# Smaller booked times for VectorE in a kernel whose instruction order is made by a planner

## The chip, the cores and the metric

The kernel runs on one core of one Trainium2 chip. The time is device microseconds of one execution; the median of several executions is given, and one further execution was taken by the hardware profiler. A core has the engines TensorE (PE in the profile; its weight loads are PEld), VectorE (DVE), ScalarE (ACT), GpSimd (POOL) and SyncE (SP, which here only issues DMAs). Each engine works off its own queue in order and waits on semaphores where it needs another engine's result. So the order in which a program writes its instructions into the queues is part of its speed.

## The reference

A block of a Flamingo model: gated cross-attention of `x` (4 x 256 x 512) to a context (4 x 1601 x 512), with 32 query heads in 8 groups of 4, head size 128, and then a gated feed-forward layer with eight low-rank experts of which two are used. All in float32.

```python
def xattn(query, kv, Wq, bq, Wkv, bkv, Wo, bo):      # 32 heads, 8 kv heads, HDIM = 128
    q = (query @ Wq + bq).reshape(B, L, NKV, G, HDIM)
    k_, v_ = jnp.split(kv @ Wkv + bkv, 2, axis=-1)
...
    scores = jnp.einsum('blkgd,bmkd->bkglm', q, k) * scale
    attn = jax.nn.softmax(scores, axis=-1)
    o = jnp.einsum('bkglm,bmkd->blkgd', attn, v).reshape(B, L, NHEAD * HDIM)
    return o @ Wo + bo

def ffn(x, base_W, router_W, lora_A, lora_B):        # E = 8, R = 16, TOP_K = 2
    base = jnp.einsum('bsd,od->bso', x, base_W)
    probs = jax.nn.softmax(jnp.einsum('bsd,ed->bse', x, router_W), axis=-1)
    top_vals, top_idx = jax.lax.top_k(probs, TOP_K)
...
    mid = jnp.einsum('bsd,edr->bser', x, lora_A) * w_dense[..., None]
    return base + jnp.einsum('bser,erd->bsd', mid, lora_B) * SCALING

x = x + jnp.tanh(g_xattn[0]) * xattn(layernorm(x), ctx_4096, ...)
x = x + jnp.tanh(g_ffn[0]) * ffn(layernorm(x), ...)
```

## The kernel before

**Tiles.** The work runs over 4 batches, 8 head groups of each, and 2 blocks of 128 queries of each group: 64 tiles. A tile (`key` = batch, head group, query block) has 4 heads x 128 queries = 512 columns. Its 1601 keys come as 13 row tiles: the remainder of 65 rows first, then six pairs of 128 rows, so 7 pieces `j` in all.

**One tile.** For each piece `score_unit` (L1109 on) writes the score product `sc` (L1138), ScalarE's copy of it from its bank into `p` (L1147), and VectorE's running maximum, by `fold`: the first pair of pieces by L1067, the short piece by L1070, the others by L1073. Then `softmax` (L1160 on) writes the spread of the maximum over the partitions (`spread`, L1078 on: L1102, L1103, L1085, L1086, L1087, L1093, L1096) and puts into queues, for each piece, the subtraction of the maximum (VectorE, L1177), the exponential (ScalarE, L1180) and the running sum (VectorE, again `fold`). `av_unit` writes the product `av` with the values (L1229); `normalize` (L1288) multiplies by the reciprocal of the sum; the output product `po` (L1306), or its seven-product form `pox`, `poy`, `poz` (L484, with VectorE's additions into `xa`, L490), follows.

`run_group(cur, prev)` alternates the score pieces of one tile with the `av` pieces of the tile before it. Between two such groups `window` fills in other work: the projections of queries, keys and values of later head groups (`pair_steps`, seven products in place of eight, names `pxq`, `pxk`, `pxv` and so on, with ScalarE's copies L941 and L944 and VectorE's additions in `add_to`, L951), the sums of weights which these products need (`weight_sums`, L351: S1, then S2 from S1, then S4 from S2, and S3 from none of them), the output products, the transposition of the next batch's context (`ctx_steps`, with VectorE's L723), and near the end the feed-forward layer.

**The planner.** The program that writes the queues keeps a clock for each engine: `clock["now"]` for TensorE, `clock["v"]` for VectorE, `clock["a"]` for ScalarE, in nanoseconds of its own reckoning. Each VectorE instruction is booked with a figure. Where it is written at once, `vec(ns)` adds the figure to `clock["v"]`; where it goes to a queue, `later(queue, "v", ns, ready, fn, key)` stores it, and `take` adds it when the piece is written. Behind a booked end `SEM` = 200 ns are added before another engine is reckoned to see the result (`done[key]`), and a PSUM bank is given back (`give`) at such a time.

Decisions made from these clocks:

- `spend` moves TensorE's clock and calls `pump`, which writes all queued pieces whose booked start lies before it; `fit` writes queued pieces that would be over by a given time, with 300 ns of tolerance (`FIT`); `force` writes what is needed for a key, with pieces in front of it that fit (1200 ns for subtractions).
- `window` picks among the tasks by when their inputs and a bank are booked to be ready. After `softmax` a time `clock["hold"]`, which is 1500 ns behind the booked end of the spread less three score products, sets up to when ready tasks are taken as filler.
- `score_unit` takes one of nine `p` buffers, whose former content must have been summed (`force(("sum", ...))`).

No figure is seen by the chip: each instruction is the same whatever is booked for it, and the semaphores guard each dependence. SP's queue is written in the same pass: `keep` stores summed weights (behind VectorE's sums), `load_pair` and `load_wo` load the next ones, booked at 6000 ns.

## Time and profile before

| what | value |
|---|---|
| median of 3 runs | 2561.35 us (2560.31 to 2561.53) |
| the profiled execution's own time | 2559.67 us |
| its span, first to last instruction | 2557.9 us |
| granted TensorE clock | 1.000 |
| VectorE busy, 1800 to 2400 us | 530.63 of 600 us |
| ScalarE busy, 1800 to 2400 us | 286.77 of 600 us |
| TensorE busy, 1200 to 1800 us | 600.00 of 600 us |

Mean durations of the VectorE groups whose booked figures change, as the groups by line and shape give them:

| line, operation | count | mean ns of one |
|---|---|---|
| L1073, maximum of a pair, 128x1024 | 252 | 1224 |
| L1073, sum of a pair, 128x1024 | 252 | 1221 |
| L1067, first maximum, 128x1024 | 63 | 1221 |
| L1070, short piece, 65x512 | 64 | 689 |
| L1177, subtraction, 65x512 | 64 | 672 |
| L1288, normalising, 128x512 | 64 | 684 |
| L351, weight sum of `wq`, 128x256 | 64 | 419 |
| L490, addition of `pox` to `xa`, 128x256 | 80 | 481 |
| L951, addition to `v`, 128x384 | 30 | 553 |

A mean duration is from an instruction's start to its end. The distance from one start to the next start can be shorter or longer than that, and is read from a timeline. A timeline's row gives the start in us, the length in us, the engine, the line, the operation, out<-in, the shapes and how many instructions were merged into the row; in brackets stands the engine's idle time before it and what ended it.

### The profile page before, as it was taken

To read this page: it belongs to the slowest core of one execution; us is meant where nothing else is said; L and a number is where in the kernel's file an instruction comes from. 1 tells how busy PE (TensorE), PEld (TensorE's weight loads), DVE (VectorE), ACT (ScalarE), POOL (GpSimd) and SP (SyncE) were. 2 spreads that over 40 slices of the span, in tenths; PEclk is the share of its full clock that TensorE was granted. 3 is DMA by queue.
4 is the path that set the end of the run, shared out by engine and by line. 5 is a ranking of instruction groups with operands and counts; after the bars stand their busy time and mean duration, and the time that the engine had idled before them with its cause. 6 is when DMAs were issued, how large, how long until landed. Compare 5 with 4: busy or idle time off the path is not lost.

```text
span 2557.9 us, 25738 instructions
## 1 busy us (share of the span) xinstructions
PE 2547.1 (100%) x9235; PEld 1486.4 (58%) x9235; DVE 2178.9 (85%) x3180; ACT 1188.1 (46%) x1899; POOL 74.4 (3%) x153
## 2 busy tenths in 40 slices
PE   9999999999999999999999999999999999999999
PEld 7557566565555656455565665756656455555544
DVE  4888898898889988999787787878788898888887
ACT  2544354445445554455444444444454445444451
POOL 0000000000000000000000000000000000000000
PEclk9999999999999999999999999999999999999999
DMA  4313222324110111012121111212221011110100
GB/s 158 122 64 108 87 102 78 113 85 149 48 56 23 44 52 56 25 39 83 50 80 37 62 52 62 81 48 81 86 83 56 26 51 52 52 50 30 49 1 33
DMA packets 75496, 167.13 MB, mean 65 GB/s; under 512 B 5372, under 2 KB 32028, under 8 KB 72808
## 3 DMA queue, kind: packets, MB, share of 16 engines
q1 hardware_dynamic: 74424, 164.41, 19.2%
q8 instruction: 73, 1.20, 0.2%
q0 software_dynamic: 416, 0.81, 0.1%
q14 instruction: 55, 0.45, 0.1%
q10 hardware_dynamic: 528, 0.26, 0.0%
HBM read 119.06 MB, written 46.40 MB: 65 GB/s over the span
## 4 chain that ended last, share of the span: by engine, by line
PE 98%; DVE 1%; DMA 0%; ACT 0%; issue 0%; SPq 0%; DVEq 0%
PE av L1229 28%; PE sc L1138 28%; PE pxk L896 6%; PE pxv L907 6%; PE pxq L896 4%; PE po L1306 3%; PE pyk L896 3%; PE pyv L907 3%; PE pox L484 3%; PE pyq L896 2%; PE pzk L896 2%; PE pzv L907 2%; PE poy L484 1%; PE pzq L896 1%; PE ptv L1020 1%; PE pv L847 1%
## 5 line engine op out<-in xcount | busy, mean ns | idle before, releaser
L1147 ACT COPY p<-sc 65x512 f32<-65x512 f32 x820 | 474.5, 586 | 658.9 <-PE sc L1138 592.1
L1138 PE MATMUL sc<-qT,kT 128*128 128x512 f32 (+1 forms) x1664 | 775.7, 592 | 0.0
L1229 PE MATMUL av<-p,v 65*128 65x512 f32 x1640 | 766.4, 592 | 2.4 <-ACT p L1180 2.4
L1229 PEld LDWEIGHTS av<-p,v 65*128 65x128 f32 x1640 | 309.2, 190 | 375.9 <-issue 367.7
L1138 PEld LDWEIGHTS sc<-qT,kT 128*128 128x128 f32 (+1 forms) x1664 | 307.0, 186 | 375.1 <-issue 342.2
L1177 DVE TENSOR_TENSOR p<-p,mb 65x512 f32<-65x512 f32 x442 | 484.4, 1137 | 0.2
L1073 DVE TENSOR_TENSOR mx<-mx,p 128x1024 f32<-128x1024 f32 x252 | 308.4, 1224 | 167.8 <-ACT p L1147 164.5
L1180 ACT ACTIVATE p<-p 65x512 f32<-65x512 f32 x442 | 421.1, 990 | 34.8 <-DVE p L1177 32.7
L1073 DVE TENSOR_TENSOR sm<-sm,p 128x1024 f32<-128x1024 f32 x252 | 307.6, 1221 | 8.6 <-DVE sm L1073 0.5
L1093 POOL COPY quadm_sm<-quadm_sm 32x16 f32<-32x16 f32 x124 | 66.0, 532 | 2302.6 <-DVE quadm_sm L1205 2298.8
L896 PE MATMUL pxq<-xq,wq 128*128 128x256 f32 x512 | 131.2, 379 | 0.0
L941 ACT ACTIVATE kT<-pxk,biasT 128x384 f32<-128x384 f32 (+1 forms) x120 | 58.0, 509 | 148.8 <-PE pxk L896 148.4
L896 PEld LDWEIGHTS pxq<-xq,wq 128*128 128x128 f32 x512 | 92.1, 189 | 30.3 <-issue 14.0
L941 ACT ACTIVATE qT<-pxq,biasT 128x256 f32<-128x256 f32 x64 | 30.3, 473 | 140.2 <-PE pxq L896 140.2
L896 PE MATMUL pxk<-T,wk 128*128 128x417 f32 (+1 forms) x240 | 90.4, 499 | 0.0
L907 PE MATMUL pxv<-wv,T 128*128 128x128 f32 x720 | 90.2, 275 | 0.0
L907 PE MATMUL pxv<-wv,ctxT 128*128 128x128 f32 x720 | 90.2, 275 | 0.0
L896 PE MATMUL pxk<-ctxT,wk 128*128 128x417 f32 (+1 forms) x240 | 90.0, 499 | 0.0
L907 PEld LDWEIGHTS pxv<-wv,ctxT 128*128 128x128 f32 x720 | 86.4, 192 | 4.2 <-issue 3.8
L907 PEld LDWEIGHTS pxv<-wv,T 128*128 128x128 f32 x720 | 86.3, 192 | 3.7 <-issue 3.3
L1067 DVE TENSOR_TENSOR mx<-p,p 128x1024 f32<-128x1024 f32 x63 | 76.9, 1221 | 12.7 <-ACT p L1147 12.1
L1306 PE MATMUL po<-wo,oT 128*128 128x512 f32 x176 | 78.5, 592 | 0.0
(264 smaller groups left out, 2674.2 us busy)
## 6 DMA issues: line engine op xcount, KB each, us to landing
wo<-in_L_xattn_Wo_dram SPq DMA_DIRECT2D x18, 1024.0 KB, 5.6
kept_q<-wq SPq DMA_DIRECT2D x16, 896.0 KB, 4.8
wq<-kept_q SPq DMA_DIRECT2D x16, 896.0 KB, 5.1
wo<-kept_wo SPq DMA_DIRECT2D x13, 1024.0 KB, 6.0
wk<-kept_k SPq DMA_DIRECT2D x11, 896.0 KB, 4.5
wv<-kept_v SPq DMA_DIRECT2D x11, 896.0 KB, 4.5
ctx<-in_ctx_dram SPq DMA_DIRECT2D x36, 256.0 KB, 2.7
wq<-in_L_xattn_Wq_dram SPq DMA_DIRECT2D x32, 256.0 KB, 3.1
```

Of the source, the lines that this page charges most:

```text
L484: nc.tensor.matmul(bk[:, :HD], left[i]()[:, c, :], blk[:, c, :], start=first and c == 0, stop=c == 1, skip_group_check=True,)
L896: nc.tensor.matmul(bk[:, :n], a(SLOT[i], c), operand(i, c, s, n), start=first and c == 0, stop=c == 1, skip_group_check=True,)
L907: nc.tensor.matmul(bk[:, t * HDIM : (t + 1) * HDIM], operand(i, c, s + t * P, P), a(SLOT[i], c), start=first and t == 0 and c == 0, stop=c ...
L941: nc.scalar.activation(dst, src, AF.Identity, bias=bias_of(kind, h0 + f))
L1067: nc.vector.tensor_tensor(acc, p[first], p[first + 1], op)
L1073: nc.vector.tensor_tensor(acc, acc, p[j], op)
L1138: nc.tensor.matmul(sc[:r, :], kT_t[b, h][:, key_col(i) : key_col(i) + r], qT_t[b, h][:, :, l * P : (l + 1) * P], start=True, stop=True,)
L1147: nc.scalar.copy(p[:r, k, :], sc[:r, :])
L1177: nc.vector.tensor_tensor(p, p, m, ALU.subtract)
L1180: nc.scalar.activation(p, p, AF.Exp, scale=scale)
L1229: nc.tensor.matmul(av, v_t[b, h][:r, i, :], p_t[key][j][:r, k, :], start=(j == 0 and k == 0), stop=(j == NPAIR - 1 and k == len(pairs[j]) ...
L1306: nc.tensor.matmul(po, oT_t[key][:, g, :], w_t["o", b, h][:, g, :], start=(g == 0), stop=(g == G - 1),)
```

## The change

Eight lines of booked figures become smaller. Nothing else in the program is touched.

```diff
@@ weight_sums
-                "T", "v", 420, clock["now"] + LAG_PAIR,
+                "T", "v", 345, clock["now"] + LAG_PAIR,
@@ block_out_steps
-                t = done[key] = vec(420)
+                t = done[key] = vec(405)
@@ add_to
-                t = vec(140 + 1.04 * src.free_size(), ready)
+                t = vec(75 + 1.04 * src.free_size(), ready)
@@ fold
-                return 1930
+                return 1870
...
-        return 1220
+        return 1150
@@ softmax
-            later("sub", "v", 1140 if n > 1 else 690, clock["v"], sub, ("sub", key, j))
+            later("sub", "v", 1140 if n > 1 else 600, clock["v"], sub, ("sub", key, j))
...
-            ns = 0 if j <= first else 1230 if j > first + 1 else 1970 if first else 1230
+            ns = 0 if j <= first else 1190 if j > first + 1 else 1870 if first else 1190
@@ sum_spread
-        later("norm", "v", 690, ("av", key), lambda: normalize(key), ("norm", key))
+        later("norm", "v", 610, ("av", key), lambda: normalize(key), ("norm", key))
```

The figures that `fold` returns are used for the maximum alone; for the sum the figures of `softmax` are booked. The figures of the spread, of the subtraction of a full pair (1140), of the sums over the context and of the block sums (L462) stay.

## The prediction

> **What bounds the kernel now.** I read the page's chain of waits first, then TensorE's waits alone, then the timelines of TensorE and VectorE. The chain ended last on TensorE for 98% of its length:

> ```profile
> PE 2547.1 (100%) x9235; PEld 1486.4 (58%) x9235; DVE 2178.9 (85%) x3180; ACT 1188.1 (46%) x1899; POOL 74.4 (3%) x153
> PE 98%; DVE 1%; DMA 0%; ACT 0%; issue 0%; SPq 0%; DVEq 0%
> ```

> Busy time alone could hide short stalls, since a matmul's recorded end overlaps the next. So I took TensorE's start-to-start distances: a 512-column matmul follows another after a median 429 ns (3,611 of them), 256 columns 216 ns (1,560), 417 columns 349 ns (444), 384 columns 322 ns (452), 128 columns 112 ns (3,074), 136 columns 115 ns (64). Counts times these medians, with the few smaller forms, are about 2541 us. TensorE ran from 1.05 to 2553.97, so 2553 us: some 12 us are not work, and 6 of them lie in the first 100 us. The listed waits agree:

> ```profile
> PE av L1229 <- ACT p L1180: 2.4, 2, 1.2
> PE pt_ctx L258 <- DMA ctx<-in_ctx_dram: 1.6, 2, 1.2
> PE warm L1791 <- DVE ones L1788: 1.1, 1, 1.1
> PE pk L803 <- ACT ctxT L260: 0.8, 1, 0.8
> PE pk L803 <- DVE ctxT L264: 0.6, 1, 0.6
> PE su L1253 <- DVE sm L1073: 0.3, 1, 0.3
> PE pmt L1540 <- DVE tail_w L1529: 0.2, 1, 0.2
> ```

> The columns are the total, the count and the longest, in us. 7.0 us in all. The reader is to see how little any new order can win: only the first two rows (without 0.4 us at 6.06) and the last two lie after the start-up, 4.1 us together. By start-to-start distances they are 4.9, and 5.1 with 0.2 in front of a block product at 2047.

> How far VectorE's work lies ahead of TensorE is the second thing. An `av` product needs the exponentials of its tile, made by VectorE's subtraction (L1177) and ScalarE's exponential (L1180). A tile in the middle of the run:

> ```profile
> 1637.68 1.23 DVE L1073 TENSOR_TENSOR mx<-mx,p 128x1024 f32<-128x1024 f32 x1 [2.21 <-ACT p L1147]
> 1638.94 0.69 DVE L1102 TENSOR_TENSOR mx<-mx 128x512 f32<-128x512 f32 x1
> ...
> 1645.21 0.68 DVE L1288 TENSOR_TENSOR oT<-av,rb 128x512 f32<-128x512 f32 x1
> 1645.80 0.41 DVE L951 TENSOR_TENSOR qT<-pyq,qT 128x256 f32<-128x256 f32 x1
> ...
> 1649.95 3.49 DVE L1177 TENSOR_TENSOR p<-p,mb 128x1024 f32<-128x1024 f32 x3
> ...
> 1654.27 0.42 DVE L462 TENSOR_TENSOR xa<-xa,oT 128x256 f32<-128x256 f32 x1
> 1654.61 0.55 DVE L951 TENSOR_TENSOR v<-pyv,v 128x384 f32<-128x384 f32 x1
> ...
> 1660.99 3.88 DVE L1073 TENSOR_TENSOR sm<-sm,p 128x1024 f32<-128x1024 f32 x3
> ```

> and ScalarE and TensorE beside it:

> ```profile
> 1644.32 1.56 ACT L1180 ACTIVATE p<-p 65x512 f32<-65x512 f32 x2
> 1662.63 1.02 PE L1229 MATMUL av<-p,v 65*128 65x512 f32 x2
> ```

> The tile's exponentials begin at 1644.3, the product that reads the first starts at 1662.6. Pairing the n-th exponential with the n-th `av` over all 64 tiles, the first product's margin has a median of 12.8 us; only two tiles have none (0.05 us), the last tile has 1.35, one has 3.7, and the rest 6.5 or more. The two bare ones are here, with what stands before them:

> ```profile
> 1190.10 3.60 PE L1306 MATMUL po<-wo,oT 128*128 128x512 f32 x8
> 1193.78 2.74 PE L1138 MATMUL sc<-qT,kT 128*65 128x512 f32 x6
> 1197.72 1.12 PE L1229 MATMUL av<-p,v 65*128 65x512 f32 x2 [1.20 <-ACT p L1180]
> ```

> ```profile
> 2434.82 1.12 PE L1229 MATMUL av<-p,v 65*128 65x512 f32 x2 [1.20 <-ACT p L1180]
> ```

> **The change, part by part.** No instruction is added or removed; eight lines of figures by which the program's writer books VectorE's time become smaller. What the chip does changes only through the order in which instructions were written into the three queues. Engine work therefore changes by 0.

> How much is booked less, for one 128-row query tile of one head group: maximum, first pair 1930 to 1870 (60), four further pairs by 70 (280); short subtraction 690 to 600 (90); sums, first 1970 to 1870 (100), four more by 40 (160); normalising 690 to 610 (80). Together 770 ns; for 63 tiles 48.5 us, or 2% of VectorE's 2178.9 us. Beside this, 75 ns on each of 96 weight sums (7.2 us), 15 on each of 140 block additions (2.1 us), 65 on each of some 300 pair additions (20 us).

> Are the new figures near the distances? Independent neighbours: subtractions in the row of three stand (3.49 - 1.22) / 2 = 1.135 us apart with 1.22 each (booked 1140, unchanged); 1645.21 to 1645.80 is 0.59 (booked 610); 1654.27 to 1654.61 is 0.34 (booked 345). Dependent ones are longer: the three sums stand (3.88 - 1.22) / 2 = 1.33 us apart, booked 1190; 1637.68 to 1638.94 is 1.26, booked 1150, for the last maximum before its spread. A tile is thus under-booked by 4 x 0.14 + 0.11 = 0.67 us at the upper end; at the lower, with 1.26 for each sum, by 0.39. In the old booking the same sums gave 4 x 0.10 + 0.04 = 0.44 and 0.16.

> [...]

> Under-booking costs time only where TensorE arrives before the result. For the tiles' exponentials the margin hides it: 0.67 us against 3.7 or more for 61 of 64 tiles. With the cover gone it costs at most 0.67 us at each of three tiles, 2.0 us. I take 0.3, as the order at those places must also turn out worse for it to count. The weight sums are chains of three and one free operation: 0.45 us chained (1653.82 to 1654.27 in the same timeline, a pair of the same size) against 345, so two of them make the last one 0.21 late, and its own 0.42 of length is 0.07 over the figure; the writer adds 200 ns behind every VectorE result, which leaves 0.08. Were 0.21 bare in all 24 groups it would be 5.0 us; I take 0.1, since the row nearest to it, TensorE's waits, shows none today on a weight sum.

> Banks are given back earlier in the booking, so a matmul that reuses one can wait. A 384-column addition is booked at 474 + 200, and its row lasts 0.55: it still ends 0.12 before the booked time. Bounds: 0 to 0.1 us for each dependent step that loses its slack; I take 0.

> SP's queue is in order and stores the summed weights behind VectorE's last sum, with loads behind them. The stored and loaded weights take 4.5 to 6.0 us to land by the page's DMA rows, booked 6.0. A sum that is put later makes the loads late by as much, a microsecond at most (one 1.22 us operation in front); I take 0, as TensorE waits for no weight load today; bounds 0 to 1.2 for one place.

> The existing waits: bounds -4.1 (the two `av` waits and the context tile of 591.13, 1.37, 1.37 and 1.38 by start-to-start distances) to 0. What ends them is the real chain from the last maximum to the exponential, and a DMA, which no booked figure shortens; I take 0. At the end of the run, where one 0.75 us addition in front of the last routing chain moves the end: -0.2 to +0.7, taken 0.1.

> Sum: 0 + 0.3 + 0.1 + 0 + 0 + 0 + 0.1 = +0.5 us. The profiled execution took 2559.67 us (span 2557.9, 1.8 around it), so 2560.2; the median of the runs shown, 2561.35, is 1.7 above that execution, so 2561.9 is the forecast against the median.

> **The rivals.** First, slower: **the cover of the short windows is moved away.** The windows between tiles close when VectorE is booked to be done; booked earlier, they take less filler, and the order of the filler changes. At 1197.72 the wait is 1.37 us although eight `po` matmuls (3.43 us) stand before it; put elsewhere, the wait becomes 4.8. The other bare tile and the one with 3.7 us of margin (its `av` at 1089.64) are the further places. Two losses of 3.43 make +6.9, so 2568.2; three 2571.6. It decides from 5.1 us of lost cover. For it: filler is scarce exactly there. Against: filler that is not taken early remains for later windows, the total is the same, and 61 tiles have 3.7 us or more in hand.

> Second, faster: **the waits after the start-up close**, because saved filler reaches the bare tiles and the context load gets more lead. All of them are -5.1, so 2556.2; two of the three long ones are -2.7, 2558.6, which is still no difference. For it: each is a mere 1.4 us. Against: it needs every one of them and no new one.

> Third, the change does not do what it says: shifts of 15 to 90 ns are smaller than the tolerances of 300 and 1200 ns with which the writer fits pieces in, so TensorE's order is hardly touched: 2561.4.

> **How the numbers follow.** A measurement of this kernel tells about 0.2%, 5.1 us, from no change. No difference, my forecast and the third rival together: 0.75. Slower, by the first rival: 0.17. Faster, by the second: 0.08. The likeliest case's own range is 2556.2 to 2566.5. For 8 in 10 I cut its lower end to 2557.5, as two of three waits would have to close for less, and reach into the first rival to 2568.5, its price for two places.

> **What would show it.** VectorE's busy time stays at 2179 us within 3, with another order. TensorE's total listed wait stays between 4 and 11 us, and its start-to-start sum at 2541. The medians of the `av` margins shift by under 3 us. I am wrong if TensorE shows new waits of over 5 us in total on an exponential, a weight sum or a context tile, or if a tile with 6.5 us of margin today is bare; the first rival is shown by a shorter run of filler in front of a bare tile.

## The result, and the profile after

Over 21 runs each, the changed kernel takes 2565.2 us (2563.58 to 2566.35) and the kernel before 2559.99 us (2559.16 to 2562.89). The ratio is 1.0019, with a 95% interval of 1.0012 to 1.0025: slower by 5.2 us, clear of zero and about as large as the 0.2% that the prediction called no difference. The profiled execution of the changed kernel took 2565.99 us, its span is 2564.2, 6.3 more than before. One execution of the run `undo_w` below, the profiled one, was slow (2667.27 us at a granted clock of 0.948); the other ten of that run have a median of 2563.4 us.

The page's first and fourth part, of the kernel after:

```profile
PE 2552.2 (100%) x9235; PEld 1487.6 (58%) x9235; DVE 2179.4 (85%) x3180; ACT 1188.1 (46%) x1897; POOL 69.1 (3%) x153
PE 96%; DVE 2%; DMA 1%; ACT 0%; issue 0%; SPq 0%; DVEq 0%; ACTq 0%
```

The same instructions, the same VectorE time (2179.4 against 2178.9), and TensorE is still the chain. TensorE's waits, total, count and longest in us:

```profile
PE av L1229 <- ACT p L1180: 2.2, 2, 1.8
PE warm L1791 <- DVE ones L1788: 1.1, 1, 1.1
PE pt_ctx L258 <- DMA ctx<-in_ctx_dram: 0.9, 1, 0.9
PE pk L803 <- ACT ctxT L260: 0.8, 1, 0.8
PE pv L847 <- DMA wv_first<-in_L_xattn_Wkv_dram: 0.8, 1, 0.8
PE pk L803 <- DVE ctxT L264: 0.5, 1, 0.5
PE pyk L896 <- ACT kT L941: 0.5, 1, 0.5
PE av L1229 <- ACT p_last L1180: 0.4, 1, 0.4
PE pmt L1540 <- DVE tail_w L1529: 0.2, 1, 0.2
```

They sum to 7.4 us, 0.4 more than before. So this view does not show where 6.3 us went. Two things escape it: a wait that begins while the last matmul's recorded end still runs, and a matmul that is simply slower. Distances from one matmul's start to the next start show both. The table gives, in us, by how much they exceed the median distance of each width, for all excesses over 15 ns (the medians themselves add up to 2540.9 us of work):

| place on TensorE | before | after | after_hold | after_hold_fit |
|---|---|---|---|---|
| start-up, to 62 us | 5.64 | 6.77 | 5.38 | 5.32 |
| `av` and `sc` in the middle | 3.10 | 4.09 | 0.34 | 0.34 |
| block products `pox`, `poy` | 1.03 | 4.06 | 4.07 | 2.15 |
| projections `pyk`, `pxq`, `pxk`, `pyq` | 0.02 | 1.49 | 1.45 | 1.47 |
| context tile (`pt_ctx`) | 1.40 | 0 | 0 | 0 |
| end, from 2480 us | 1.05 | 2.20 | 2.19 | 2.19 |
| other (`pt_base`) | 0.09 | 0.09 | 0.09 | 0.09 |
| sum without start-up | 6.7 | 11.9 | 8.1 | 6.2 |
| measured median against before | | +5.2 | +1.2 | -1.1 |

The last two columns are experiments told below. The start-up row is taken as chance: TensorE's order there is the same, and among the profiles it lies between 5.3 and 9.0; TensorE's wait for the first load of `wv_first`, for one, is 0.8 us in the kernel after and 1.6 in `dep`, and the kernel before has none. Without it the sums differ by 5.2 us, which is the difference of the medians; with it by 6.4, about the difference of the two profiled executions (6.3).

**The place at 1200 us.** TensorE after, at the tile whose `av` product waited before too:

```profile
1196.92 2.74 PE L1138 MATMUL sc<-qT,kT 128*65 128x512 f32 x6
1199.50 0.41 PE L258 MATMUL pt_ctx<-ident,ctx 65*128 65x65 f32 x4
1201.68 1.12 PE L1229 MATMUL av<-p,v 65*128 65x512 f32 x2 [1.77 <-ACT p L1180]
1202.65 3.46 PE L1138 MATMUL sc<-qT,kT 128*128 128x512 f32 x4
1205.90 2.04 PE L1229 MATMUL av<-p,v 128*128 128x512 f32 x4
```

The eight `po` matmuls that stood here are gone, the wait is 1.77 in place of 1.20, and the four score matmuls behind it take 3.46 us, where four take 1.88 elsewhere. The granted clock was not in the prediction. The view by windows (after the window and its length: TensorE, weight loads, VectorE, ScalarE and GpSimd busy, each with its count, then the granted clock, the DMA share and GB/s):

```profile
1203.00:1207.00 4.00, 4.00 (x7) 1.62 (x6) 4.00 (x5) 3.85 (x5) 0.00 (x0) 0.60 0.00 0
```

The clock's record in the trace has half speed from 1202.80 to 1206.21, 3.41 us. By the distances, the wait costs 1.94 and the half clock 1.70 us, 3.6 together, against 1.4 before.

Why the output product was gone: it became ready one window earlier. Its tile's normalising on VectorE, before and then after:

```profile
1164.11 0.69 DVE L1288 TENSOR_TENSOR oT<-av,rb 128x512 f32<-128x512 f32 x1
```

```profile
1157.57 0.68 DVE L1288 TENSOR_TENSOR oT<-av,rb 128x512 f32<-128x512 f32 x1
```

Before, the next tile's scores began at 1162.51, so the product was not ready in the window in front of them and was written a window later. After, it was ready, and the window took it with the one before:

```profile
1162.47 7.03 PE L1306 MATMUL po<-wo,oT 128*128 128x512 f32 x16
```

What set the length of the wait stands on ScalarE. The product needs the exponential of the short piece (L1180), and that needs VectorE's subtraction (L1177). Before:

```profile
1192.93 0.69 DVE L1177 TENSOR_TENSOR p<-p,mb 65x512 f32<-65x512 f32 x1
1196.55 0.58 ACT L1147 COPY p<-sc 128x512 f32<-128x512 f32 x1 [0.27 <-PE sc L1138]
1197.04 5.37 ACT L1180 ACTIVATE p<-p 65x512 f32<-65x512 f32 x6
```

The subtraction was over at 1193.62, but the exponential began 3.4 us later, behind ScalarE's copies of the next tile's scores, which wait for the score matmuls. So the `po` matmuls in front of those scores did not shorten this wait: they moved the scores, the copies and the exponential together. After:

```profile
1199.13 7.50 DVE L1177 TENSOR_TENSOR p<-p,mb 65x512 f32<-65x512 f32 x7
1199.70 0.58 ACT L1147 COPY p<-sc 128x512 f32<-128x512 f32 x1 [0.27 <-PE sc L1138]
1200.80 0.30 ACT L754 COPY ctxT<-rest 128x132 f32<-128x132 f32 x1
1201.01 1.57 ACT L1180 ACTIVATE p<-p 65x512 f32<-65x512 f32 x2
```

The short piece, the first of its row, was over at 1199.82; the exponential began 1.2 us later, behind the score copies and behind three copies of the context tile (L260, L752, L754), whose transposition had moved behind the scores.

**The block products.** VectorE before, near 204 us:

```profile
203.49 1.67 DVE L351 TENSOR_TENSOR wq<-wq 128x256 f32<-128x256 f32 x4
205.15 0.48 DVE L490 SCALAR_TENSOR_TENSOR xa<-poy,gates,xa 128x256 f32<-128x256 f32 x1
206.01 0.48 DVE L490 SCALAR_TENSOR_TENSOR xa<-pox,gates,xa 128x256 f32<-128x256 f32 x1 [0.38 <-PE pox L484]
```

and after, with TensorE beside it:

```profile
205.43 1.33 DVE L351 TENSOR_TENSOR wq<-wq 128x256 f32<-128x256 f32 x3
206.68 0.48 DVE L490 SCALAR_TENSOR_TENSOR xa<-poy,gates,xa 128x256 f32<-128x256 f32 x1
207.08 0.41 DVE L351 TENSOR_TENSOR wq<-wq 128x256 f32<-128x256 f32 x1
```

```profile
206.07 1.03 PE L484 MATMUL pox<-xa,xa 128*128 128x256 f32 x4
207.21 1.13 PE L484 MATMUL poy<-xa,oT 128*128 128x256 f32 x4
```

Before, the four weight sums were over when the first `poy` product ended, and the addition followed at once. After, three of them stand in front of it; the first `poy` product ended as `pox` began at 206.07, but its addition starts at 206.68. The next product into the same bank waits for it: 207.21 in place of 206.07 + 0.86 = 206.93, 0.28 us late, and the idle time is only 0.1 beyond the former matmul's recorded end. A second gap of 0.10 follows inside the product that waited. There are 21 places with such waits (35 gaps), 4.1 us in all. At five of them a weight sum stands directly in front of the addition, as here (1.4 us); at nine it is a tile's running sum (L1070 or L1073), at seven its normalising (L1288).

### The profile page after: what moved, and what is told of

Its sections match the earlier page's. It is cut to its first block, busy times and chain, and to the rows that moved or that the text cites. A ratio compares the mean times of both kernels' runs of the same rounds, so it can differ in the third digit from the quotient of the medians.

```text
span 2564.2 us, 25799 instructions
## 1 busy us (share of the span) xinstructions
PE 2552.2 (100%) x9235; PEld 1487.6 (58%) x9235; DVE 2179.4 (85%) x3180; ACT 1188.1 (46%) x1897; POOL 69.1 (3%) x153
## 4 chain that ended last, share of the span: by engine, by line
PE 96%; DVE 2%; DMA 1%; ACT 0%; issue 0%; SPq 0%; DVEq 0%; ACTq 0%
PE sc L1138 28%; PE av L1229 27%; PE pxk L896 6%; PE pxv L907 6%; PE pxq L896 4%; PE po L1306 3%; PE pyk L896 3%; PE pyv L907 3%; PE pox L484 3%; PE pyq L896 2%; PE pzk L896 2%; PE poy L484 1%; PE pzv L907 1%; PE pzq L896 1%; PE ptv L1020 1%; PE py L1478 1%
## 5 line engine op out<-in xcount | busy, mean ns | idle before, releaser
L1147 ACT COPY p<-sc 65x512 f32<-65x512 f32 x820 | 477.4, 585 | 684.9 <-PE sc L1138 644.1
L1138 PE MATMUL sc<-qT,kT 128*128 128x512 f32 (+1 forms) x1664 | 777.7, 593 | 0.0
L1229 PE MATMUL av<-p,v 65*128 65x512 f32 x1640 | 766.5, 593 | 2.2 <-ACT p L1180 2.2
L1229 PEld LDWEIGHTS av<-p,v 65*128 65x128 f32 x1640 | 309.8, 190 | 378.3 <-issue 370.1
L1138 PEld LDWEIGHTS sc<-qT,kT 128*128 128x128 f32 (+1 forms) x1664 | 307.4, 186 | 372.8 <-issue 342.5
L1177 DVE TENSOR_TENSOR p<-p,mb 65x512 f32<-65x512 f32 x442 | 484.7, 1138 | 0.5
L1073 DVE TENSOR_TENSOR mx<-mx,p 128x1024 f32<-128x1024 f32 x252 | 308.3, 1223 | 188.0 <-ACT p L1147 184.5
L1180 ACT ACTIVATE p<-p 65x512 f32<-65x512 f32 x442 | 420.5, 990 | 43.3 <-DVE p L1177 40.4
L1073 DVE TENSOR_TENSOR sm<-sm,p 128x1024 f32<-128x1024 f32 x252 | 307.6, 1221 | 11.2
L1093 POOL COPY quadm_sm<-quadm_sm 32x16 f32<-32x16 f32 x124 | 60.7, 490 | 2313.4 <-DVE quadm_sm L1205 2309.6
L944 ACT COPY v<-pxv 128x384 f32<-128x384 f32 x90 | 42.9, 476 | 80.4 <-PE pxv L907 79.9
```

Of the source, the lines that this page charges most:

```text
L1073: nc.vector.tensor_tensor(acc, acc, p[j], op)
L1138: nc.tensor.matmul(sc[:r, :], kT_t[b, h][:, key_col(i) : key_col(i) + r], qT_t[b, h][:, :, l * P : (l + 1) * P], start=True, stop=True,)
L1147: nc.scalar.copy(p[:r, k, :], sc[:r, :])
L1177: nc.vector.tensor_tensor(p, p, m, ALU.subtract)
L1180: nc.scalar.activation(p, p, AF.Exp, scale=scale)
L1229: nc.tensor.matmul(av, v_t[b, h][:r, i, :], p_t[key][j][:r, k, :], start=(j == 0 and k == 0), stop=(j == NPAIR - 1 and k == len(pairs[j]) ...
```

## The experiments

Each run was measured together with the kernel before, on the same chip. Medians in us:

| run | this | before | difference | ratio, 95% interval |
|---|---|---|---|---|
| undo_w | 2563.59 | 2560.58 | +3.0 | 1.0012 (1.0003 to 1.0021) |
| only_w | 2561.56 | 2560.58 | +1.0 | 1.0004 (0.9995 to 1.0014) |
| only_tile | 2561.08 | 2560.58 | +0.5 | 1.0002 (0.9993 to 1.0011) |
| only_ba | 2564.78 | 2560.58 | +4.2 | 1.0018 (1.0010 to 1.0027) |
| after_fill | 2564.02 | 2560.08 | +3.9 | 1.0015 (1.0006 to 1.0024) |
| after_fit | 2563.14 | 2560.08 | +3.1 | 1.0014 (1.0005 to 1.0023) |
| after_both | 2562.31 | 2560.08 | +2.2 | 1.0009 (1.0000 to 1.0018) |
| only_b | 2560.59 | 2560.08 | +0.5 | 1.0002 (0.9993 to 1.0011) |
| after_hold | 2561.60 | 2560.37 | +1.2 | 1.0006 (0.9997 to 1.0015) |
| after_hold_fit | 2559.29 | 2560.37 | -1.1 | 0.9996 (0.9988 to 1.0005) |
| dep | 2562.39 | 2560.37 | +2.0 | 1.0007 (0.9998 to 1.0016) |
| a_180 | 2561.75 | 2560.37 | +1.4 | 1.0004 (0.9995 to 1.0013) |

The intervals are some 2.3 us to either side, and eight of the twelve reach or include a ratio of 1. So single differences under that, and differences between two runs, prove little by their times; what supports them is the excess by place, read as in the table above. In each run but `undo_w` its sum without the start-up (and with 1.8 us for added matmuls where there are some) gives the measured difference within 1.0 us.

**First, which figure.** The changed kernel without the weight sums' figure:

```diff
-                "T", "v", 345, clock["now"] + LAG_PAIR,
+                "T", "v", 420, clock["now"] + LAG_PAIR,
```

> The changed kernel with the weight sums' figure back at 420. Theory W (chained weight sums, booked 345 where they stand 0.45 us apart, are put ahead of the block additions of L490, so that the block products pox and poy wait): TensorE's waits before pox and poy fall from 4.1 us to about the 1.0 of before, and the time is some 3 us under the changed kernel (about 2562). Rival T (the figures of the tiles, maximum and sum, decide what stands ahead of the additions): those waits stay near 4 us, and the time stays at about 2565.

2.2 us of the 5.2 went (2.4 by the ten other executions), nearer to theory W. Its only profile has an excess of 0.72 us at the block products; TensorE's granted clock was 0.948 there, against 0.999 in the kernel after, so that is a hint for theory W and no proof. The same figure alone on the kernel before:

> The kernel before with the weight sums' figure alone at 345. Theory W: the waits before pox and poy rise from 1.0 to about 4 us, time about 2563. Rival T: they stay near 1 us, time about 2560. Both: the wait of the av product at about 1198 us stays at 1.2 to 1.4, with no drop of the granted clock behind it.

+1.0 us, and the excess before `poy` and `pox` rose from 1.03 to 2.10, not to 4: the figure does this, but about a third of it alone. The tiles' figures alone (`fold`, the short subtraction, the sums, normalising, as in the change):

> The kernel before with the tiles' figures alone changed (maximum, short subtraction, sum, normalising). Theory W: block product waits near 1 us; the av wait at about 1200 us grows to 1.9 with a stretch of half clock behind it, and the wait of the last tile appears (1.4), so +2 to +4 us: 2562 to 2564. Rival T: block product waits near 4 us as well, time about 2565.

The half clock came as expected (idle 1.78, then 3.41 us of half clock), and the block products stayed at 1.26, so rival T falls. But the time rose by 0.5 only, under theory W's +2 to +4: the wait at 2434.82 us of before closed (-1.4), and the end of the run has 0.3 in place of 1.05. The two addition figures alone (`vec(405)`, `75 + 1.04 n`):

> The kernel before with the block additions (405) and the pair additions (75 + 1.04 n) alone changed. Theory W and rival T: neither concerns these, the time stays within 1.5 us of before (2558.5 to 2561.5). A third view, that any small shift of the order costs, since the order of before has unusually few waits: +2 to +5 us here too, with waits at other places.

+4.2: both theories missed this, and the third view's time held, though not its other places. TensorE's waits of this run, the largest:

```profile
PE av L1229 <- ACT p L1180: 2.5, 1, 2.5
PE pt_ctx L258 <- DMA ctx<-in_ctx_dram: 2.3, 3, 1.2
```

It is the same place, at 1202.45, with the output product moved in the same way, an idle time of 2.51 and half clock behind it (4.3 us by the distances). Here the exponential began at 1201.76, just after its subtraction's end at 1201.73, so VectorE ended this wait. Block products had 1.93. The four runs show that no one figure holds the loss. The parts do not add either: +1.0, +0.5 and +4.2 make 5.7, but each comes with other places, and the parts share the place at 1200.

**Then, what each place costs.** Eight small matmuls (16 in the profile's count) in the place of the idle time:

```diff
+        fill = 8 if (j, key) == (0, (1, 6, 1)) else 0
...
+        [nc.tensor.matmul(av[:, :P], ident, ident, start=True, stop=True) for _ in range(fill)]
```

> The changed kernel with eight small matmuls (identity by identity, about 0.22 us each, overwritten by what follows) in front of the av product that waits 1.8 us at about 1200 us. No other instruction moves. Theory C (the wait itself is only part of the price; a TensorE that idles 1.8 us is granted half the clock for the next 3.41 us, which costs 1.7 us): the wait of that product stays as long counted from the transposition before it, no stretch of half clock follows, and the time is 1.5 to 1.9 us under the changed kernel, about +3.5 us against before. Rival C (the half clock is hidden, since what follows waits for VectorE's subtractions anyway): the time stays at about +5 us.

The window that had a clock of 0.60:

```profile
1203.00:1207.00 4.00, 4.00 (x11) 1.73 (x10) 3.96 (x5) 3.74 (x4) 0.00 (x0) 1.00 0.00 0
```

No half clock, and the `av` product still starts 2.19 us after the transposition (2.18 before this edit). The time fell by 1.3 us (+5.2 to +3.9), not by 1.7. Theory C holds for the clock; of its price 0.6 us was given back at 1226 us, where the projections now wait for VectorE:

```profile
1226.52 1.13 PE L896 MATMUL pxq<-xq,wq 128*128 128x256 f32 x4 [0.47 <-DVE qs_q L951]
```

Less tolerance in front of the block additions:

```diff
-                fit("v", clock["now"] + SEM)
+                fit("v", clock["now"] + SEM - FIT)
                 part = xa_t[b][:, l, d * HD : (d + 1) * HD]
```

> The changed kernel, but in front of a block addition (L490) only such VectorE pieces are fitted as end 300 ns sooner; on TensorE next to nothing moves. Theory W (what delays pox and poy is a VectorE piece fitted in front of the addition that their bank waits for): TensorE's waits before pox and poy fall from 4.1 to under 1 us and the time by about 3 us, to +2 against before. Rival W (the additions are late because VectorE is behind altogether): the waits stay above 2.5 us and the time within 1 us of the changed kernel.

-2.1 us, and the excess of the block products fell from 4.06 to 2.20. On VectorE, at the place shown above, two sums are left in front of the addition:

```profile
206.44 0.87 DVE L351 TENSOR_TENSOR wq<-wq 128x256 f32<-128x256 f32 x2
207.27 0.48 DVE L490 SCALAR_TENSOR_TENSOR xa<-poy,gates,xa 128x256 f32<-128x256 f32 x1
```

So the fitted pieces are the cause for some 60% of the rise of 3.0, and neither theory's bound was met. At the five places with a weight sum directly in front nothing waits any more; at nine of the ten places that still wait a tile's running sum stands in front of the addition. What put it there was not traced.

> Both edits on the changed kernel. If theories C and W hold and their prices add: 1.7 + 3 us under the changed kernel, within 1.5 us of before (-1 to +1.5). If either rival holds: +2 to +4.

+2.2, so 3.0 us under the changed kernel, where the single edits gave 1.3 and 2.1. The two prices about add, but neither is as large as expected, and the time itself lies in the range that was given for the rivals. What shows that both edits work is the places: no half clock, and 2.21 us at the block products.

> The kernel before with the block additions' figure alone (420 to 405). TensorE's order stays as it is, a few VectorE instructions change places. Theory A (the loss of the two addition figures together, +4.2 us, comes from the pair additions, whose figure falls by 65 on some 300 instructions): this stays within 0.7 us of before. Rival A (15 ns are enough): +2 us or more, with new waits before pox or poy.

+0.5, inside theory A's bound. TensorE's order is that of before but for one `pox` product, put earlier (1411 in place of 1419 us), and 38 of VectorE's 3,180 places differ. Yet the block products have 1.98 us in place of 1.03, as much as in `only_ba`, 0.63 of it in one wait of a `poy` product: the new waits of rival A came, at less than half its price. The rest of the loss of `only_ba` is thus put down to the pair additions, by difference; they were not shortened in a run of their own.

**Last, the cover put back.** The output product held back by one window:

```diff
-                steps = out_steps(prev)
+                steps = [] if prev == (1, 5, 1) else out_steps(prev)
+                if prev == (1, 6, 0): tasks.insert(0, Task(out_steps((1, 5, 1))))
```

> The changed kernel, with one output product (eight po matmuls of batch 1, head group 5, second query block) held back by one window, to the place that it has in the kernel before: in front of the tile whose av product waits at about 1200 us. Theory P (the price at that place is moved cover: the output product ran one window earlier): no wait of that product over 0.3 us, no half clock behind it, and 2 to 3.6 us under the changed kernel (1.9 of wait and 1.7 of half clock, less up to 1.5 given back where TensorE next waits for VectorE): +1.6 to +3.2 against before. Rival P (VectorE is later there by itself, through the under-booking): the wait stays over 1 us and the time within 1 us of the changed kernel.

TensorE of this run:

```profile
1192.13 3.60 PE L1306 MATMUL po<-wo,oT 128*128 128x512 f32 x8
1195.57 0.41 PE L258 MATMUL pt_ctx<-ident,ctx 65*128 65x65 f32 x4
1195.81 2.74 PE L1138 MATMUL sc<-qT,kT 128*65 128x512 f32 x6
1198.39 1.02 PE L1229 MATMUL av<-p,v 65*128 65x512 f32 x2
```

No wait at all, no half clock, and 4.0 us of the 5.2 are gone, a little more than theory P's upper end. All other places are as in the changed kernel, so the place of this one task of 3.43 us decides the price here. But it is not only cover, since before the same task stood there and the product waited. ScalarE of this run:

```profile
1195.12 0.63 ACT L1180 ACTIVATE p<-p 65x512 f32<-65x512 f32 x1 [2.20 <-DVE p L1177]
```

The exponential now stands in front of the copies, directly behind its subtraction (over at 1195.03). No run moves ScalarE's order alone, so how the 3.6 us of this place divide between the task's time and that order stays open. Nor is it the largest part of what the change cost: against before the place had lost 2.2 us, the block products 3.0; the edit regains more because the old wait of 1.4 goes too.

> The same with the tighter fitting in front of the block additions. If theories P and W hold and add: about 4 to 5.5 us under the changed kernel, -0.5 to +1.2 against before, with no TensorE wait over 1 us left in the middle of the run. If one of the rivals holds: +2 to +3.5.

-1.1 us against before, 6.3 under the changed kernel, somewhat better than was expected of both together (by place -0.4): theories P and W add. TensorE's largest waits of this run are those of the start-up:

```profile
PE warm L1791 <- DVE ones L1788: 1.1, 1, 1.1
PE pk L803 <- ACT ctxT L260: 0.8, 1, 0.8
PE pk L803 <- DVE ctxT L264: 0.5, 1, 0.5
PE pyk L896 <- ACT kT L941: 0.5, 1, 0.5
```

It has the lowest median of all the kernels here, but its interval (0.9988 to 1.0005) does not tell it from the kernel before.

**Is it under-booking, or only another order?** Chained operations booked at chained distances:

```diff
-                "T", "v", 345, clock["now"] + LAG_PAIR,
+                "T", "v", 450 if out_ in (S1, S2) else 345, clock["now"] + LAG_PAIR,
...
-        return 1150
+        return 1260 if j == NPAIR - 1 else 1150
...
-            ns = 0 if j <= first else 1190 if j > first + 1 else 1870 if first else 1190
+            ns = 0 if j <= first else 1260 if j > first + 1 else 2040 if first else 1260
```

(The test on S1 and S2 lengthens S1 and S2, the two that the next one waits for.)

> The changed kernel, but with chained operations booked at their chained distances: 450 for the weight sums S2 and S4's forerunners, 1260 for the sums and the last maximum, 2040 for the first sum. Theory U (the loss is systematic under-booking of chained VectorE work): most of the loss goes, 0 to +1.5 against before. Rival R (the loss is that of another order as such: before's order has few waits, and any shift of figures gives new places): +2 to +5 again, with waits at other places or the same.

+2.0, outside theory U's bound and at the lower end of rival R's. The block products fell to 0.69 us, less than before's 1.03: theory U holds for them, although three figures were changed at once and `undo_w` points the same way with the old figure of 420. The place at 1200 stayed (idle 2.52, 4.3 us by the distances; the exponential at 1203.69 just after its subtraction's end at 1203.66), with the output product a window early again (16 `po` matmuls from 1163.88): rival R holds there. And longer pair additions on the kernel before:

```diff
-                t = vec(140 + 1.04 * src.free_size(), ready)
+                t = vec(180 + 1.04 * src.free_size(), ready)
```

> The kernel before with the pair additions booked longer by 40 (180 + 1.04 n) in place of shorter by 65. Theory U: longer figures leave TensorE more in hand, so no new waits: within 1 us of before. Rival R: +1.5 to +5, as for the shorter figures.

+1.4, between what theory U allows and rival R's lower end, and too near to both for its interval to decide, with other waits in front of block products (2.5 us in place of 1.0) and none at the context tile. So a shift of either sign moved waits about; how much of that is chance among orders stays open after two samples.

## Why the prediction was right or wrong

The range held the time (2557.5 to 2568.5 against 2565.2), and the difference, which was to stay under 5.1 us, came out at 5.2: on the edge, not at +0.5. That is luck: the forecast missed the difference by 4.7 us, the range held because it reached up to the first rival's price for two places, and most of what filled it had no such term. Step by step:

- **The bound was right.** TensorE's work by distances is 2540.9 us in both kernels, VectorE's busy time moved by 0.5, the median margin of the `av` products went from 12.8 to 13.9 us, and the listed waits are 7.4 us, within 4 to 11. The last test was a poor one: the loss is not in that list. And the waits of before outside the start-up were 6.7 us, not 5.1, when gaps down to 15 ns are counted.
- **The tiles' exponentials, taken 0.3, at most 2.0.** The mechanism of the sum was wrong: at the place at 1200 us the subtraction was done 1.2 us before its exponential began, so VectorE's lateness did not set the wait. What came was the first rival's lost output product at the place that it named, in the size of 2.2 us net (3.6 against 1.4). Its price was mis-sized on both sides. The wait became 1.9 us, not 4.8, since the exponential stood behind the copies of the next scores: without the `po` matmuls those scores came sooner, and the exponential with them. And the half clock behind it, 1.7 us, was no term at all.
- **The weight sums, taken 0.1 because TensorE's waits show none today on a weight sum.** This failed. The step asked who waits for a weight sum, and not what is queued behind one on VectorE: the block additions. "I take 0" for the banks failed with it. Measured: +3.0 us on the block products, of whose 4.1 us weight sums stand directly in front of 1.4 and a tile's sums or normalising of the rest.
- **The existing waits, bounds -4.1 to 0, taken 0.** Two of the three long ones closed, the context tile's at 591.13 and the `av` wait at 2434.82: about -2.8, as the second rival had it, against new ones of 8. The reason given for 0, that the real chain from the last maximum to the exponential ends the `av` waits, was wrong: in the kernel before, the exponential began 3.4 us (at 1197.04) and 0.6 us (at 2434.14) after its subtraction's end, in both cases behind ScalarE's copies of the next scores. So the order that the planner writes does set these waits.
- **The end, -0.2 to +0.7, taken 0.1.** It was +1.15, outside the bounds. Not an addition in front of the routing chain, but the exponentials of the last tile: its `av` products wait 0.62 and 0.60 us. On VectorE a routing chain (L1384 to L1395, from 2483.32) now stands in front of that tile's last maximum (2487.53); before, it came after the tile's subtractions (from 2492.84). This was not tried by a run of its own.
- **The projections** had no term and cost 1.5 us, 0.65 of it in one wait of a `pyk` product for ScalarE, which had a table load (1.28 us, from 1049.86) and an exponential (0.63 us) in front of the copy. Nor was this tried.
- **The third rival** (TensorE's order hardly touched) fell: from 166.8 us on, TensorE's order differs at 1,713 or more of its 9,235 places, and `only_b` shows that 15 ns are enough to change VectorE's.

## What to carry to other kernels

Where TensorE is full, look for a loss in its start-to-start distances, not in its listed idle time: 35 gaps of 0.03 to 0.28 us made 4 us here and hardly showed. When a planner's figure is shortened, ask what it puts in front of instructions that a PSUM bank waits for, and compare the figures of chained operations with chained distances. When a result gets ready earlier, its consumer may leave the one place where it did good; holding one task back regained 4 of 5 us. And when a product waits for an exponential, look at what stands in front of that exponential in ScalarE's queue before putting the wait down to VectorE.
